# Two graph layers on one core: attention addends moved from TensorE transposes to a VectorE block transpose and two DMAs, row biases folded into beta, planner steps re-timed

## The chip, the core and the metric

The kernel runs on one core of a Trainium2 chip. The metric is the device time of one execution in microseconds. The kernel before took 3455.34 us, the median of three runs (3453.7 to 3455.74). The execution that was profiled took 3450.98 us; its trace spans 3449.2 us from the first to the last instruction.

## The reference

64 graphs of 256 nodes with 256 features go through two layers, all in fp32. Layer 0 is two graph attentions (GAT), a residual layernorm, and a feed-forward with relu. Layer 1 is attention with 8 heads whose values depend on the relation of the edge, and a feed-forward with gelu.

```python
def _gat(h, adj, W, a, out_features):
    Wh = jnp.matmul(h, W)
    Wh1 = jnp.matmul(Wh, a[:out_features])
    Wh2 = jnp.matmul(Wh, a[out_features:])
    e = jax.nn.leaky_relu(Wh1 + jnp.swapaxes(Wh2, 1, 2), negative_slope=ALPHA)
    att = jax.nn.softmax(jnp.where(adj > 0, e, NEG), axis=1)
    return jnp.matmul(att, Wh)
# layer 0
h = _gat(_gat(x, adj, W1, a1), adj, W2, a2)
h = _layernorm(x + h, g_ln1, b_ln1)
x = _layernorm(h + relu(h @ w_ff1 + b_ff1) @ w_ff2 + b_ff2, g_ln2, b_ln2)
# layer 1
attn = softmax((x @ Wq + bq) (x @ Wk + bk)^T / sqrt(32))     # per head
out = sum over r of (attn * (adj == r)) @ (x @ Wv[r] + bv[r])
x = _ln(x + out @ Wo + bo, g1, beta1)
x = _ln(x + gelu(x @ W1 + b1) @ W2 + b2, g2, beta2)
```

In a GAT layer, the weight of an edge comes from a sum of one number per row node and one per column node. The kernel calls these numbers the addends. Because exp(leaky_relu(s)) is the larger of exp(s) and exp(0.2 s), an unnormalised weight is the maximum of two products, each of a factor per row and a factor per column.

## The kernel before

**Tiling.** The 64 graphs are handled in 32 pairs. A pair has four row tiles of 128 nodes (index `k`, two per graph `b`). Each pair is a Python generator, `whole_way`, which emits the instructions of the pair in steps and yields between them. A feed-forward (`feed_forward`, L301) has eight steps that each make one 128x512 tile of the hidden layer (L308, two matmuls, with the activation at L311), and four quarters that multiply with the second weight (L319). A 128x512 fp32 matmul shows in the trace as two records.

**Order.** The order is written out by a small planner, `in_turn` (L151). Up to three pairs are under way. Each yield gives three things: the TensorE time of the step in us, the latency until the pair's next step may begin, and a stage that the next step needs. Three stages ("gat", "attention", "ff") are exclusive: only one pair may be in each. Among the pairs whose due time has come, those outside the feed-forward go first, so feed-forward steps fill the gaps. The costs in the yields only choose the order in which the program is written. On the chip each engine runs its own queue in order and waits at semaphores. The framework that assigns the semaphores may also shift an instruction against others in its engine's queue: the trace shows loads of `adjT` issued by SyncE ahead of an older output.

**The GAT stage** (`gat_layers`, L215). The projection (L227) of the pair's `xT` gives each row its 256 features and the addends in extra columns; ScalarE copies it to SBUF (L229). `addends` (L181) takes the largest absolute addend per graph (`steep`, a range check), and three exponentials on ScalarE: two of the row factor (`rise`, L189 and L190) and one of the ratio of the column factors (`ratio`, L191). `gat_weights` (L194) then needs the row factors along the free axis and on all partitions. Per graph, four TensorE transposes (L199) of a column broadcast to 128x128 put them into a PSUM bank; ScalarE copies half of it to `up` (L201); VectorE forms the maximum (L206), masks with the adjacency and sums (L207), takes the reciprocal (L209), and ScalarE scales the rows (L212). The product with the weights is L241 in the first GAT layer and L253 in the second. Then come residual and layernorm.

**Rows transposed** (`rows_transposed`, L294). Ahead of each feed-forward and of the attention, the rows are transposed on TensorE (L289), copied by ScalarE to `yT` (L290; two buffers), and GpSimd adds the bias of the coming sublayer to the rows (L292), so that the residual already holds it. The generator first takes the stage ("ff" or "attention") and then transposes.

**Layernorm** (`layernorm`, L268) is VectorE work, with the power -1/2 on GpSimd (L276).

**Transfers.** All are issued by SyncE: per pair `xT` (one buffer), `adjT` (four) and `x` (four) at L59 to L63, and the output at L456, which is written from the `x` tile. The load of the next pair is written right after the projection of the present one.

**Setup.** The weights are loaded to SBUF once; two small matmul groups (L119) fold the addend vectors into the first weight.

Of the kernel before, what the change touches and what calls it, by code (L numbers as in the profile page):

```python
# [29 lines left out]
def two_layers(ctx: ExitStack, tc: tile.TileContext, t: dict, out: bass.AP, flag: bass.AP):  # L30
# [25 lines left out]
    def load(pair):  # L56
        rows = slice(2 * pair, 2 * pair + 2)
        xT = io.tile([P, KC, 512], F32, name="xT")
        nc.sync.dma_start(xT, t["xT"][pair].rearrange("(c p) b n -> p c (b n)", p=P))  # L59
        adjT = io.tile([P, 4, N], I32, name="adjT", bufs=4)  # L60
        nc.sync.dma_start(adjT, t["adjT"][rows].rearrange("b (c p) n -> p (b c) n", p=P))
        x = io.tile([P, 4, D], F32, name="x", bufs=4)
        nc.sync.dma_start(x, t["x"][rows].rearrange("b (c p) d -> p (b c) d", p=P))  # L63
        return xT, adjT, x
# [13 lines left out]
    most = const.tile([P, NPAIR, 4], F32, name="most")  # L78
    steep = const.tile([P, NPAIR, 4], F32, name="steep")

# [23 lines left out]
    with tc.tile_pool(name="setup", bufs=1) as setup, \  # L104
            tc.tile_pool(name="psetup", bufs=2, space=bass.MemoryType.PSUM) as psetup:
        w1T, a2 = weights("L0_gnn_W1T", setup), on_all("L0_gnn_a2", 2 * D, setup)
        right = setup.tile([P, KC, D + 4], F32, name="right")
        nc.sync.dma_start(right[:, :, :D], t["L0_gnn_W2"].rearrange("(c p) m -> p c m", p=P))
        nc.sync.dma_start(right[:, :, D + 2:], t["L0_gnn_a1c"])
        junk = setup.tile([P, D], F32, name="junk")  # L110
        for s in range(2):
            for c in range(KC):
                nc.vector.scalar_tensor_tensor(
                    junk, right[:, c, :D], 1.0, a2[:, s * D:(s + 1) * D], op0=ALU.mult, op1=ALU.mult,
                    accum_out=right[:, c, D + s:D + s + 1])
        for m in range(KC):
            pw = psetup.tile([P, 512], F32, name="pw")
            for c in range(KC):
                nc.tensor.matmul(pw[:, :D + 4], lhsT=w1T[:, c, m * P:(m + 1) * P], rhs=right[:, c],  # L119
                                 start=c == 0, stop=c == KC - 1)  # L120
            nc.vector.tensor_copy(w12[:, m], pw[:, :D + 4])
    ln = [tuple(on_all(n, D) for n in names) for names in (
        ("L0_gnn_g_ln1", "L0_gnn_b_ln1"), ("L0_gnn_g_ln2", "L0_gnn_b_ln2"),
        ("L1_gnn_g1", "L1_gnn_beta1"), ("L1_gnn_g2", "L1_gnn_beta2"))]
    ff0 = (weights("L0_gnn_w_ff1"), column("L0_gnn_b_ff1"), weights("L0_gnn_w_ff2"), on_all("L0_gnn_b_ff2", D))
    wq, wk, wo = weights("L1_gnn_Wq"), weights("L1_gnn_Wk"), weights("L1_gnn_Wo")
    wv = const.tile([P, KC, 2, D], F32, name="wv")
    for c in range(KC):
        nc.sync.dma_start(wv[:, c], t["L1_gnn_Wv"][:2, c * P:(c + 1) * P, :].rearrange("r p m -> p r m"))
        nc.vector.tensor_tensor(wv[:, c, 1], wv[:, c, 1], wv[:, c, 0], ALU.subtract)  # L130
    bq, bk = column("L1_gnn_bq"), column("L1_gnn_bk")
    bqs = const.tile([P, KC], F32, name="bqs")
    nc.vector.tensor_scalar(bqs, bq, SCALE, None, ALU.mult)
    bv, bo = on_all("L1_gnn_bv", 2 * D), on_all("L1_gnn_bo", D)
    nc.vector.tensor_tensor(bv[:, D:], bv[:, D:], bv[:, :D], ALU.subtract)
    ff1 = (weights("L1_gnn_W1"), column("L1_gnn_b1"), weights("L1_gnn_W2"), on_all("L1_gnn_b2", D))

    work = ctx.enter_context(tc.tile_pool(name="work", bufs=1))
    small = ctx.enter_context(tc.tile_pool(name="small", bufs=6))
    psum = ctx.enter_context(tc.tile_pool(name="psum", bufs=8, space=bass.MemoryType.PSUM))  # L140

# [38 lines left out]

    def addends(y, at, layer, pair, b):  # L181


        k = of_graph(b)
        nc.vector.tensor_reduce(steep[:, pair, 2 * layer + b:2 * layer + b + 1], y[:, k, at:at + 2], axis=AX.XY,
                                op=ALU.max, apply_absolute_value=True)
        e1, e2 = y[:, k, at], y[:, k, at + 1]
        rise, ratio = small.tile([P, 2, 2], F32, name="rise"), small.tile([P, 2], F32, name="ratio")
        nc.scalar.activation(rise[:, 0], e1, AF.Exp, bias=shift[:, 0:1])  # L189
        nc.scalar.activation(rise[:, 1], e1, AF.Exp, bias=shift[:, 0:1], scale=ALPHA)  # L190
        nc.scalar.activation(ratio, e2, AF.Exp, scale=ALPHA - 1.0)  # L191
        return rise, ratio

    def gat_weights(y, at, rise, ratio, adjT, empty, b):  # L194

        p = bank()
        for n in range(4):
            col = rise[:, n // 2, n % 2:n % 2 + 1]
            nc.tensor.transpose(p[:, n * P:(n + 1) * P], col.to_broadcast([P, P]), ident)  # L199
        up = work.tile([P, N], F32, name="up", bufs=2)  # L200
        nc.scalar.activation(up, p[:, :N], AF.Copy)  # L201
        e = work.tile([P, 2, N], F32, name="e", bufs=4)
        sums, rs = small.tile([P, 2], F32, name="sums"), small.tile([P, 2], F32, name="rs")
        for j in range(2):
            k = 2 * b + j
            nc.vector.scalar_tensor_tensor(e[:, j], p[:, N:], ratio[:, j:j + 1], up, op0=ALU.mult, op1=ALU.max)  # L206
            nc.vector.scalar_tensor_tensor(e[:, j], adjT[:, k], empty[:, k:k + 1], e[:, j],  # L207
                                           op0=ALU.max, op1=ALU.min, accum_out=sums[:, j:j + 1])
# [6 lines left out]
    def gat_layers(pair, xT, adjT, x):  # L215
# [4 lines left out]
        z = work.tile([P, 4, D + 4], F32, name="xw", bufs=2)  # L220
        a, e = [], []
        for b in range(2):
            for j in range(2):
# [5 lines left out]
                nc.scalar.activation(y[:, k], ps[:, :D + 4], AF.Copy)  # L229
            a.append(addends(y, D + 2, 0, pair, b))  # L230
            yield 1.75, b * 1.6, None
        if pair + 1 < NPAIR:
            loaded[pair + 1] = load(pair + 1)
        for b in range(2):
            e.append(gat_weights(y, D + 2, *a.pop(0), adjT, empty, b))
            yield 0.5, b * 3.4, None
        for b in range(2):
            for i in range(2):
# [4 lines left out]
                nc.scalar.activation(z[:, 2 * b + i, :D + 2], ps[:, :D + 2], AF.Copy)  # L243
            a.append(addends(z, D, 1, pair, b))
            yield 1.75, 0.4 + b * 0.6, None
        for b in range(2):
            e.append(gat_weights(z, D, *a.pop(0), adjT, empty, b))
            yield 0.5, b * 3.4, None
        for b in range(2):
# [9 lines left out]
        done_with("gat")  # L259
        yield 1.75, 4.5, "ff"  # L260

# [21 lines left out]

    def transposed(y, yT, bias, b):

        pt = bank()
        for c in range(KC):
            for j in range(2):
                nc.tensor.transpose(pt[:, c * N + j * P:c * N + (j + 1) * P], y[:, 2 * b + j, c * P:(c + 1) * P], ident)  # L289
        nc.scalar.activation(yT[:, :, b * N:(b + 1) * N], pt.rearrange("p (c n) -> p c n", c=KC), AF.Copy)  # L290
        for j in range(2):
            nc.gpsimd.tensor_tensor(y[:, 2 * b + j, :], y[:, 2 * b + j, :], bias, ALU.add)  # L292

    def rows_transposed(y, bias):  # L294
        yT = work.tile([P, KC, 512], F32, name="yT", bufs=2)
        for b in range(2):
            transposed(y, yT, bias, b)
            yield 0.5, 0.5 + b * 0.5, None
        return yT

    def feed_forward(y, w, func, gb):  # L301
        w1, b1, w2, b2 = w
        yT = yield from rows_transposed(y, b2)
        f = []
# [40 lines left out]
    def attention(y, pair, adjT):  # L345


        yT = yield from rows_transposed(y, bo)
        qT, kT, oT = (work.tile([P, KC, 512], F32, name=n) for n in ("qT", "kT", "oT"))

# [73 lines left out]
        for n, (b, c) in enumerate(groups):  # L424
# [9 lines left out]
            divided(b, c, po)  # L434
            yield 3.1 if last else 4.1, 3.2 if last else 0.8, None
            if (b, c) == (0, KC - 1):
# [8 lines left out]
        done_with("attention")  # L445
        yield 1.75, 4.5, "ff"

    def whole_way(pair):
        yield 0.0, 0.0, "gat"
        xT, adjT, x = loaded.pop(pair)  # L450
        yield from gat_layers(pair, xT, adjT, x)
        yield from feed_forward(x, ff0, AF.Relu, ln[1])
        yield 3.44, 4.5, "attention"
        yield from attention(x, pair, adjT)
        yield from feed_forward(x, ff1, AF.Gelu, ln[3])
        nc.sync.dma_start(out[2 * pair:2 * pair + 2].rearrange("b (c p) d -> p (b c) d", p=P), x)  # L456
        yield 3.44, 0.0, None

    in_turn((whole_way(pair) for pair in range(NPAIR)), 3)


    ranges = ((reach, NPAIR * 4, N * SAFE), (most, NPAIR * 4, 1.0), (steep, NPAIR * 4, STEEP))
    count = const.tile([P, len(ranges)], F32, name="count")
# [405 lines left out]

_COLUMNS = ("L0_gnn_b_ff1", "L1_gnn_bq", "L1_gnn_bk", "L1_gnn_b1")  # L870


# [24 lines left out]
```

## Time and profile before

| quantity | value |
|---|---|
| median of 3 runs | 3455.34 us |
| profiled execution, and its span | 3450.98 us, 3449.2 us |
| granted TensorE clock | 0.999 |
| TensorE busy | 3344.4 us (97%) |
| VectorE, ScalarE, GpSimd busy | 1904.6, 1371.0, 481.5 us |
| DMA traffic over the span | 22 GB/s |
| activation table loads on ScalarE | 218 of 1283 ns |

How to read it: busy times are the union of the spans of an engine's instructions. Matmuls are pipelined, so a matmul's own duration is longer than the spacing at which the next one follows; where two rows of the timeline follow without a gap, the difference of their starts is the time that counts. In a list of groups, the figures are busy time, mean duration of one, then the idle time of that engine just before them and what ended it. A wait for several semaphores is put down to the one that came last.

### The profile page before, as it was taken

How to read it: one execution, taken by the hardware profiler on the slowest of the kernel's cores; microseconds unless marked ns; L12 is line 12 of the kernel's file. 1: busy time of each engine (PE TensorE's matmuls, PEld its weight loads, DVE VectorE, ACT ScalarE, POOL GpSimd, SP SyncE). 2: the span in 40 equal slices, each digit the busy share in tenths (PEclk: the TensorE clock that was granted, in tenths of full speed). 3: DMA queues.
4: the chain of work that ended last, by engine and by line, in shares of the span. 5: the costliest groups of instructions: out<-in, count | busy, mean ns of one | idle time of the engine just before them, and what ended most of it. 6: DMA issues, size and time to landing. Idle time of an engine off the chain costs nothing.

```text
span 3449.2 us, 47284 instructions
## 1 busy us (share of the span) xinstructions
PE 3344.4 (97%) x18698; PEld 2150.5 (62%) x18698; DVE 1904.6 (55%) x4825; ACT 1371.0 (40%) x2586; POOL 481.5 (14%) x646
## 2 busy tenths in 40 slices
PE   7999999999999999999999999999999999999998
PEld 5566665666656566565665666656666566565655
DVE  5655645556456564555645555465554655546455
ACT  4343343433434334343444434444253442534332
POOL 0201111011110111111111111111111111111110
PEclk9999999999999999999999999999999999999999
DMA  5000010000100001000000100001000010000000
GB/s 166 7 25 19 13 37 7 25 19 13 37 7 25 25 7 37 7 28 23 20 25 7 41 10 25 19 7 43 7 25 19 7 43 7 25 19 1 13 1 14
DMA packets 66868, 78.22 MB, mean 23 GB/s; under 512 B 3280, under 2 KB 57680, under 8 KB 66640
## 3 DMA queue, kind: packets, MB, share of 16 engines
q1 hardware_dynamic: 66640, 75.13, 7.0%
q8 instruction: 150, 2.46, 0.3%
q14 instruction: 78, 0.64, 0.1%
HBM read 58.34 MB, written 16.78 MB: 22 GB/s over the span
## 4 chain that ended last, share of the span: by engine, by line
PE 87%; ACT 9%; DVE 2%; DMA 1%; issue 0%; SPq 0%; POOL 0%; POOLq 0%; DVEq 0%
PE ps L319 26%; PE ps L308 23%; PE ps L342 7%; PE ps L335 6%; PE ps L388 6%; PE ps L360 4%; PE ps L381 4%; PE ps L253 3%; PE ps L405 3%; ACT L189 2%; ACT yT L290 2%; PE ps L241 2%; PE ps L227 2%; PE ps L289 1%; ACT ff L311 1%; DVE e L206 1%
## 5 line engine op out<-in xcount | busy, mean ns | idle before, releaser
L276 POOL TENSOR_TENSOR rstd<-rstd,mhalf 128x2 f32<-128x2 f32 x256 | 206.1, 805 | 2729.3 <-DVE rstd L275 2713.4
L308 PE MATMUL ps<-yT,w_L_gnn_W 128*128 128x512 f32 x1024 | 482.7, 602 | 14.2 <-ACT yT L290 12.5
L308 PE MATMUL ps<-yT,w_L_gnn_w_ff 128*128 128x512 f32 x1024 | 482.5, 602 | 14.1 <-ACT yT L290 12.5
L319 PE MATMUL ps<-w_L_gnn_w_ff,ff 128*128 128x256 f32 x2048 | 450.2, 379 | 0.0
L319 PE MATMUL ps<-w_L_gnn_W,ff 128*128 128x256 f32 x2048 | 449.9, 379 | 0.0
L319 PEld LDWEIGHTS ps<-w_L_gnn_W,ff 128*128 128x128 f32 x2048 | 389.1, 190 | 66.6 <-issue 15.3
L319 PEld LDWEIGHTS ps<-w_L_gnn_w_ff,ff 128*128 128x128 f32 x2048 | 389.0, 190 | 66.0 <-issue 14.8
L374 DVE TENSOR_TENSOR m<-a,adjT 128x512 f32<-128x512 f32 x512 | 327.0, 688 | 175.6 <-ACT a L365 134.9
L266 DVE TENSOR_TENSOR x<-ps,x 128x512 f32<-128x512 f32 x256 | 176.1, 688 | 444.3 <-PE ps L319 330.7
L311 ACT ACTIVATE ff<-ps,c_L_gnn_b_ff 128x512 f32<-128x512 f32 x256 | 176.0, 687 | 448.2 <-PE ps L308 448.2
L365 ACT ACTIVATE a<-ps 128x512 f32<-128x512 f32 x512 | 264.4, 602 | 216.3 <-PE ps L360 216.1
L337 DVE TENSOR_TENSOR v<-ps,b_L_gnn_bv 128x512 f32<-128x512 f32 x128 | 88.1, 689 | 400.5 <-PE ps L335 400.5
L308 PEld LDWEIGHTS ps<-yT,w_L_gnn_W 128*128 128x128 f32 x1024 | 183.0, 190 | 199.2 <-issue 174.1
L308 PEld LDWEIGHTS ps<-yT,w_L_gnn_w_ff 128*128 128x128 f32 x1024 | 183.1, 190 | 198.9 <-issue 174.2
L290 ACT ACTIVATE yT<-ps 128x512 f32<-128x512 f32 x192 | 110.2, 592 | 479.8 <-PE ps L289 479.8
L311 ACT ACTIVATE ff<-ps,c_L_gnn_b 128x512 f32<-128x512 f32 x256 | 175.9, 687 | 292.8 <-PE ps L308 292.4
L335 PE MATMUL ps<-wv,yT 128*128 128x512 f32 x512 | 235.4, 592 | 0.0
L229 ACT ACTIVATE xw<-ps 128x260 f32<-128x260 f32 x128 | 45.7, 379 | 456.0 <-PE ps L227 456.0
L394 DVE RECIPROCAL s<-ps 128x256 f32<-128x256 f32 x128 | 224.0, 1750 | 0.0
L273 DVE BATCH_NORM_STATS2 st<-x 128x6 f32<-128x256 f32 x512 | 192.7, 418 | 8.6
L206 DVE SCALAR_TENSOR_TENSOR e<-ps,ratio,up 128x256 f32<-128x256 f32 x256 | 115.7, 475 | 141.2 <-ACT up L201 141.2
L335 PEld LDWEIGHTS ps<-wv,yT 128*128 128x128 f32 x512 | 97.3, 190 | 122.5 <-issue 122.2
(81 smaller groups left out, 4290.1 us busy)
## 6 DMA issues: line engine op xcount, KB each, us to landing
xT<-in_xT SPq DMA_DIRECT2D x32, 512.0 KB, 4.6
adjT<-in_adjT SPq DMA_DIRECT2D x32, 512.0 KB, 3.9
x<-in_x SPq DMA_DIRECT2D x32, 512.0 KB, 4.2
out<-x SPq DMA_DIRECT2D x32, 512.0 KB, 3.2
w_L_gnn_w_ff<-in_L_gnn_w_ff SPq DMA_DIRECT2D x2, 1024.0 KB, 11.3
w_L_gnn_W<-in_L_gnn_W SPq DMA_DIRECT2D x2, 1024.0 KB, 7.0
wv<-in_L_gnn_Wv SPq DMA_DIRECT2D x2, 256.0 KB, 7.1
w_L_gnn_W1T<-in_L_gnn_W1T SPq DMA_DIRECT2D x1, 256.0 KB, 6.1
```

The lines of the kernel that those rows point to most:

```text
L273: nc.vector.bn_stats(st[:, j, :], r[:, 2 * b + j, :])
L276: nc.gpsimd.tensor_tensor(rstd, rstd, mhalf[:, :2], ALU.pow)
L290: nc.scalar.activation(yT[:, :, b * N:(b + 1) * N], pt.rearrange("p (c n) -> p c n", c=KC), AF.Copy)
L308: nc.tensor.matmul(p1, lhsT=w1[:, c, m * P:(m + 1) * P], rhs=yT[:, c, :], start=c == 0, stop=c == KC - 1)
L311: nc.scalar.activation(h, p1, func, bias=b1[:, m:m + 1])
L319: nc.tensor.matmul(p2[:, j * D:(j + 1) * D], lhsT=f[m][:, k * P:(k + 1) * P], rhs=w2[:, m, :], start=m == 0, stop=m == NF - 1)
L335: nc.tensor.matmul(ps, lhsT=yT[:, c, at:at + P], rhs=wv[:, c].rearrange("p r m -> p (r m)"), start=c == 0, stop=c == KC - 1)
L342: nc.tensor.matmul(ps, lhsT=w[:, d, c * P:(c + 1) * P], rhs=yT[:, d, :], start=d == 0, stop=d == KC - 1)
L365: nc.scalar.activation(a, ps[o], AF.Exp)
L374: nc.vector.tensor_tensor(m, a, adj, ALU.mult)
L388: nc.tensor.matmul(po[o * DH:(o + 1) * DH, :N], lhsT=v[:, jc, at:at + DH], rhs=ms[o][:, jc * N:(jc + 1) * N], start=r == 0 and jc == 0, st ...
L394: nc.vector.reciprocal(s, po[:, N:])
```

## The change

Five things are edited together.

- **Addends.** Both graphs of the pair are handled by one call. The four row factors are written into a 128x64 tile (`rise`, two of them, cleared once), VectorE transposes it in 32x32 blocks, a first DMA writes 4 KB of the result to a DRAM scratch tile, and a second DMA reads them back onto all 128 partitions (`rows`, 4 KB on each). `gat_weights` reads `rows` in place of PSUM and of `up`. The four TensorE transposes and the ScalarE copy per graph are gone.
- **Row biases.** The three row biases are added to the beta of the layernorm in front, at setup. What else reads those rows would then see the bias too, so it is taken out of the biases of the readers (`b1`, `bq`, `bk`, `bv`) with small matmuls at setup. GpSimd's adds per pair are gone.
- **Row transposes** no longer need the stage; it is asked for after them. `yT` has three buffers.
- **Latencies** in the yields are changed, and the weights steps cost no TensorE time.
- **Loads.** The next pair's load is written after the second layer's addends, `x` has five buffers, and the output is written one yield later.

```diff
-        x = io.tile([P, 4, D], F32, name="x", bufs=4)
+        x = io.tile([P, 4, D], F32, name="x", bufs=5)
...
+        for n, (name, readers) in enumerate((("L0_gnn_b_ff2", ((ff0[0], ff0[1]),)),
+                                             ("L1_gnn_bo", ((wq, bq), (wk, bk))),
+                                             ("L1_gnn_b2", ((ff1[0], ff1[1]),)))):
+            beta = ln[n][1]
+            nc.vector.tensor_tensor(beta, beta, on_all(name, D, setup), ALU.add)
+            b = setup.tile([P, KC], F32, name="c_" + name)
+            nc.sync.dma_start(b, t[name + "c"])
+            for w, bias in readers:
+                pw = psetup.tile([P, 512], F32, name="pw")
+                of = w.shape[-1] // P
+                for m in range(of):
+                    for c in range(KC):
+                        nc.tensor.matmul(pw[:, m:m + 1], lhsT=w[:, c, m * P:(m + 1) * P], rhs=b[:, c:c + 1],
+                                         start=c == 0, stop=c == KC - 1)
+                nc.vector.tensor_tensor(bias, bias, pw[:, :of], ALU.subtract)
...
+        rise, ratio = rises[layer], small.tile([P, 4], F32, name="ratio")
+        of_kind = rise.rearrange("p j (n s) -> p n j s", n=4)[:, :, :, 0]
+        for b in range(2):
+            e1 = y[:, of_graph(b), at]
+            nc.scalar.activation(of_kind[:, 2 * b], e1, AF.Exp, bias=shift[:, 0:1])
+            nc.scalar.activation(of_kind[:, 2 * b + 1], e1, AF.Exp, bias=shift[:, 0:1], scale=ALPHA)
+        nc.scalar.activation(ratio, y[:, :, at + 1], AF.Exp, scale=ALPHA - 1.0)
+        blocks = small.tile([P, 2, 32], F32, name="blocks")
+        nc.vector.transpose(blocks.rearrange("p j c -> p (j c)"), rise.rearrange("p j c -> p (j c)"))
+        row = scratch.tile([2, 16, 32], F32, name="row")
+        nc.sync.dma_start(row.rearrange("j q c -> q j c"), blocks[0:P:8])
+        rows = work.tile([P, 8, 4, 32], F32, name="rows", bufs=2)
+        nc.sync.dma_start(rows.rearrange("p q n c -> p (q n c)"), row.rearrange("j q c -> (j q c)").partition_broadcast(P))
...
-        p = bank()
-        for n in range(4):
-            col = rise[:, n // 2, n % 2:n % 2 + 1]
-            nc.tensor.transpose(p[:, n * P:(n + 1) * P], col.to_broadcast([P, P]), ident)
-        up = work.tile([P, N], F32, name="up", bufs=2)
-        nc.scalar.activation(up, p[:, :N], AF.Copy)
...
-            nc.vector.scalar_tensor_tensor(e[:, j], p[:, N:], ratio[:, j:j + 1], up, op0=ALU.mult, op1=ALU.max)
+            nc.vector.scalar_tensor_tensor(e[:, j].rearrange("p (q c) -> p q c", q=8), rows[:, :, 2 * b + 1],
+                                           ratio[:, k:k + 1], rows[:, :, 2 * b], op0=ALU.mult, op1=ALU.max)
...
-            a.append(addends(y, D + 2, 0, pair, b))
-            yield 1.75, b * 1.6, None
-        if pair + 1 < NPAIR:
-            loaded[pair + 1] = load(pair + 1)
-        for b in range(2):
-            e.append(gat_weights(y, D + 2, *a.pop(0), adjT, empty, b))
-            yield 0.5, b * 3.4, None
+            if b == 0:
+                yield 1.75, 0.0, None
+        rows, ratio = addends(y, D + 2, 0, pair)
+        yield 1.75, 8.6, None
+        e = [gat_weights(y, D + 2, rows, ratio, adjT, empty, b) for b in range(2)]
+        yield 0.0, 4.6, None
...
+        rows, ratio = addends(z, D, 1, pair)
+        if pair + 1 < NPAIR:
+            loaded[pair + 1] = load(pair + 1)
+        yield 1.75, 8.6, None
+        e += [gat_weights(z, D, rows, ratio, adjT, empty, b) for b in range(2)]
+        yield 0.0, 4.6, None
...
-        yield 1.75, 4.5, "ff"
+        yield 1.75, 6.0, None
...
+    def rows_transposed(y, needs):
+
+        yT = work.tile([P, KC, 512], F32, name="yT", bufs=3)
         for b in range(2):
-            transposed(y, yT, bias, b)
-            yield 0.5, 0.5 + b * 0.5, None
+            pt = bank()
...
+            yield 0.5, 0.5 + b * 0.8, needs if b else None
...
-        yield 3.44, 4.5, "attention"
+        yield 3.44, 6.0, None
         yield from attention(x, pair, adjT)
         yield from feed_forward(x, ff1, AF.Gelu, ln[3])
+        yield 3.44, 5.0, None
         nc.sync.dma_start(out[2 * pair:2 * pair + 2].rearrange("b (c p) d -> p (b c) d", p=P), x)
-        yield 3.44, 0.0, None
```

In the attention, the step after the last group of heads is told 4.8 us in place of 3.2, and the feed-forward behind the attention 6.0 us and no stage in place of 4.5 us and "ff".

## The prediction

> **What bounds the kernel now.** I read the top of the page first, then the busy time of each engine in stretches, then TensorE's waits, then TensorE's timeline, and last the rows that price the pieces.
>
> ```profile
> span 3449.2 us, 47284 instructions
> ...
> PE 3344.4 (97%) x18698; PEld 2150.5 (62%) x18698; DVE 1904.6 (55%) x4825; ACT 1371.0 (40%) x2586; POOL 481.5 (14%) x646
> ```
>
> TensorE is busy for 97%, and no other engine for more than 55%. So only two things can shorten the run: less streaming on TensorE, or fewer gaps. The gaps are 3449.2 - 3344.4 = 104.8 us. Busy time by stretches shows where they lie (first column the stretch, then its length and PE's busy time):
>
> ```profile
> 0.00:45.20 45.20, 25.09 (x105) 18.95 (x105) 21.77 (x75) 15.50 (x47) 4.71 (x12) 0.96 0.93 287
> ...
> 439.00:652.40 213.40, 208.53 (x1170) 134.16 (x1169) 118.50 (x300) 85.96 (x163) 29.89 (x41) 1.00 0.07 21
> ```
>
> The first 45.2 us, up to the first feed-forward matmul, hold 20.1 us of idle. After that the work repeats every 213.4 us, which is two pairs of graphs (106.7 us each), and each period has 4.87 us of idle. TensorE's waits over the run name them (total us, times, longest):
>
> ```profile
> PE ps L199 <- ACT rise L189: 29.6, 46, 0.9
> PE ps L308 <- ACT yT L290: 25.0, 34, 0.7
> PE ps L253 <- ACT xw L212: 21.0, 16, 3.0
> PE pw L119 <- DVE junk L113: 11.4, 1, 11.4
> ```
>
> All but L119 recur per pair: the transposes of the addend columns (L199) wait for ScalarE's exponentials, the feed-forward (L308) for the copy of its transposed rows, the GAT product (L253) for the scaled rows. TensorE's timeline over one GAT stage shows them in place:
>
> ```profile
> 1078.45 1.04 PE L289 MATMUL ps<-ident,x 128*128 128x128 f32 x8
> 1079.32 0.60 PE L199 MATMUL ps<-ident,rise 128*128 128x128 f32 x4
> 1080.44 0.65 PE L199 MATMUL ps<-ident,rise 128*128 128x128 f32 x4 [0.52 <-ACT rise L189]
> 1081.21 3.70 PE L308 MATMUL ps<-yT,w_L_gnn_W 128*128 128x512 f32 x8
> ...
> 1091.66 0.60 PE L199 MATMUL ps<-ident,rise 128*128 128x128 f32 x4
> 1093.18 0.65 PE L199 MATMUL ps<-ident,rise 128*128 128x128 f32 x4 [0.92 <-ACT rise L189]
> ```
>
> Starts matter here, not durations: eight L289 transposes last "1.04", but the next group starts 0.87 after them. A transpose occupies the stream for 0.109 us, and the remaining 0.17 us is a drain that overlaps the next work, or is lost in front of a gap.
>
> **What the skill says.** "TensorE: Matmul & The Clock Gate", Part 4, gives about 275 ns for a PE transpose inside a kernel and says that access latency dominates it. The trace agrees in duration (76.3 us of union over 512, 277 ns mean in the PE groups), but the price of taking one away is the spacing, 0.109 us. "DMA: Bandwidth & Descriptors", Two DMAs through the same engine are not ordered: the second of the two new DMAs has to wait for the first one's completion, so their latencies add. No run here shows this yet. The same page, Latency and other measured facts, puts a DMA's fixed cost near 2 us, mostly the write receipt; the 512 KB output here lands in 3.2 us, which fits. "ScalarE: Activation LUTs", What ACT_TABLE_LOAD costs: 1283 ns; the trace has 1283 too. (Prices used below besides: a VectorE 128x128 transpose, 311 ns for bf16, "VectorE: DVE Perf Modes", The three transpose paths.)
>
> ```profile
> adjT<-in_adjT SPq DMA_DIRECT2D x32, 512.0 KB, 3.9
> x<-in_x SPq DMA_DIRECT2D x32, 512.0 KB, 4.2
> out<-x SPq DMA_DIRECT2D x32, 512.0 KB, 3.2
> ```
>
> **The change, part by part.** The sum is made against the profiled execution, 3450.98 us (span 3449.2 and 1.8 around it). The median of the runs, 3455.34, is 4.4 above it.
>
> *Transposes out of TensorE.* 4 transposes x 2 graphs x 2 layers x 32 pairs = 512, at 0.109 us: **-55.7 us**, all on the bounding engine. The 128 `up` copies (42.7 us of ScalarE) and 64 of 128 `ratio` exponentials go too; ScalarE is busy for 40%, so they count only through waits.
>
> *The steady gaps.* 4.87 us per period, plus the drain lost in front of each gap (19 waits in the 650 us from 800 to 1450, so 6.2 per period, x 0.17 = 1.06), is 5.93, or 2.97 per pair. The L199 wait goes with its instructions. The L290 wait goes because the rows are transposed before the stage is free, behind other steps (third `yT` buffer). The L212 wait goes because the planner is told 4.6 us between weights and product and fills it. Over about 31 pairs: **-92 us**. This leaves 106.7 - 2.97 - 16 x 0.109 = 102.0 us per pair.
>
> *What comes late next.* The new chain, from the end of the projection to the first product: ACT copy 0.39, table load 1.28, five exponentials at their spacing of 0.19 (1.05 with the last), maximum 0.15 and transpose 0.25 on VectorE (between the 0.15 of the small reduction and the 0.31 of the page), first DMA 2.5 (4 KB; between the page's 2.0 and the 3.2 of the 512 KB output), second DMA 4.0 (512 KB into SBUF; the loads take 3.9 and 4.2; bounds 3.2 and 5.5 with other traffic), then two L206, two L207, reciprocal and two L212 for the first graph, 3.1. Sum 12.7. I walked the planner's rule with the new costs for the order of the steps only. In the steady order, five L308 steps and two quarters of L319 stand between the first layer's addends and its product: 5 x 1.72 + 2 x 3.45 = 15.5 us of cover. A load of `xT` becomes due at the same moment (the projection frees its buffer) and is 1.4 us of transfer at the 370 GB/s of the start: 14.1, still covered; a layernorm half on VectorE (about 3 us) in front would uncover 1.6. In the second layer some 30 us of the next attention's first steps are cover. But there the row scaling (L212) stands on ScalarE behind the rows' landing, and the feed-forward's activation and the next attention's `yT` copies queue behind it. By the same sums the rows land about 9.3 us after the projection while these activations come from 8 us on, so up to 1.7 us reaches TensorE at the first attention projection. I take 0.4 for the first place and 0.9 for the second, 1.3 per pair (bounds 0.3 and 5): 31 x 1.3 = **+40 us**.
>
> *SyncE's queue.* Per pair four small issues of about 0.4 us come in. They'd be stuck if they stood behind a waiting transfer. The `adjT` wait (L61) and the output wait (L456) make up nearly all of SP's waiting before. In the new order the output is issued before the next pair's projection, told 8.4 us after its layernorm; the `adjT` and `x` buffers of a new load (x now has five) are free long before. I cost this at 0, because those 8.4 us cover the layernorm (about 4 us); if the output were late it would hold both row DMAs back.
>
> *Biases into beta.* 192 x 2 POOL adds go, 276 us of POOL, which waits 2729 us in front of its power operation (L276): 0 on the path, as no chain that TensorE waits for goes through them. In exchange 42 setup matmuls (84 records) come, at 0.109 to 0.19 each: 9 to 16 us, with weights as their cover at the start.
>
> *Start and end.* The first pair has no feed-forward to hide behind. Before, its first L308 starts at 45.2. Now two chains lie open. If its projection still runs at 15.8 us while the weights load (landings then take 4 to 11 us, so 14 for two instead of 6.5): 19.5 + 20 + 3.7 + 13 + 3.6 + a layernorm 4 + transposes and copy 1.5 = 66. If it has to stand behind the setup matmuls, whose last weights land after 35 us, the same sum starts at 37 to 45 and ends at 79 to 87. So +21 to +42; I take **+32**. The longer latencies at the last pair: **+4**.
>
> Sum: -55.7 - 92 + 40 + 32 + 4 = -71.7, so 3379 in the profiled execution and **3384 us** in the median.
>
> **Rivals.** (1) *Row chain late, slower.* Mechanism: TensorE takes its steps in order, so each product L241 waits if the rows land after the cover. With 3 us of layernorm ahead of the transpose, 1.5 us more in each DMA by traffic, and the ScalarE block of 1.7, the stall is 12.7 + 1.4 + 3 + 3 - 15.5 = 4.6, plus 1.7: about 6 per pair, less what doesn't coincide, 5. It decides from (147.7 - 36)/31 = 3.6 us per pair on. At 5: 3384 + 31 x 3.7 = 3499. For it: two dependent DMAs in a row where VectorE is 55% busy. Against: 1.4 to 2.8 us to spare by durations. (2) *Gaps only change names.* New stalls equal the old, 2.6 per pair: 3384 + 40 = 3424. For it: the old latencies were also told, and still 4.87 us remained per period. (3) *No new stall* (0.3) and the short start (21), no end cost: 3379 - 31 - 11 - 4 + 4 = 3337. A measurement of this kernel can tell about 0.2% (7 us) from no change. That the removed transposes don't shorten TensorE's stream I exclude, as they aren't overlapped by other matmuls in the timeline.
>
> **How the numbers follow.** Forecast (3362 to 3408) 0.60; rival 2 (3408 to 3448) 0.20; rival 3 0.07; rival 1 0.13. The range 3345 to 3440 leaves out rival 1, the lower half of rival 3 and the top of rival 2, 0.18 in all. Faster 0.84, within 0.2% 0.04, slower 0.12.
>
> **What would show it.** Right: the period (pair) falls from 106.7 to about 103.3; L199 is gone from TensorE's groups; the rows' second DMA lands in about 4 us; the waits of L308 for `yT` nearly vanish; first L308 near 77. Wrong: a wait of L241 for L212 of over 2 us per pair, or the row DMAs on SyncE behind an output or a load (rival 1); as many gaps at the attention's first projections as there were at L199 (rival 2).

## The result, and the profile after

The changed kernel takes **3457.1 us** (median of 4 runs, 3455.7 to 3458.5), the kernel before 3454.5 us beside it (3451.5 to 3455.7). The ratio of the times is 1.0009, with an interval of 0.9991 to 1.0026: no difference that can be measured. The forecast was 3384, with a range of 3345 to 3440, so the result lies outside it.

The top of the page of the kernel after:

```profile
span 3455.4 us, 45656 instructions
...
PE 3323.7 (96%) x18270; PEld 2129.3 (62%) x18270; DVE 1843.1 (53%) x4835; ACT 1261.9 (37%) x2326; POOL 202.9 (6%) x262
```

The work did go away: 428 matmul records fewer (512 transposes out, 84 setup matmuls in), 260 fewer on ScalarE, 384 fewer on GpSimd. But the span is 6 us longer, and TensorE's idle time grew from 104.8 to 131.7 us. And its busy time fell by 20.7 us only, where the transposes alone were 55.7 and the setup matmuls add 9 to 16: the rest must have become slower. The mean granted clock says so: 0.983, where it was 0.999.

TensorE's waits over the run (total us, times, longest):

```profile
PE ps L418 <- DVE v L367: 66.1, 47, 2.4
PE pw L155 <- DMA b_L_gnn_bo<-in_L_gnn_bo: 18.1, 1, 18.1
PE pw L123 <- DVE junk L117: 11.9, 1, 11.9
PE ps L272 <- ACT xw L245: 10.8, 1, 10.8
PE ps L287 <- ACT xw L245: 9.3, 1, 9.3
...
PE ps L338 <- ACT yT L327: 1.4, 2, 0.7
```

All the steady waits of before are gone. The feed-forward's wait for `yT` (L338, formerly L308) fell from 25.0 to 1.4 us, the GAT products L272 and L287 wait once each, at the start. One new wait has taken their place: the attention's product of weights and values, L418, waits for `v`, which VectorE copies with its bias at L367. The prediction names no such wait.

47 waits in 32 pairs are neither one nor two per pair. The output DMAs, as SyncE's timeline shows them, tell why (start us, duration):

```profile
1990.10 0.39 SPq L487 DMA_DIRECT2D out<-x  x1
2096.82 0.39 SPq L487 DMA_DIRECT2D out<-x  x1
2203.19 0.39 SPq L487 DMA_DIRECT2D out<-x  x1
2305.72 0.39 SPq L487 DMA_DIRECT2D out<-x  x1
```

The distance is 106.7 and 106.4 us, and then 102.5. It stays at 102.5 for all 11 distances after 2203.19. In the 18 before it, values of 106.4 to 106.7 and of 107.8 alternate, with a mean of 106.9, as slow as before the change (106.7). So the run has two halves. One period from each, as stretches (stretch, length, busy time of PE, PEld, DVE, ACT, POOL, then granted clock, DMA share, GB/s):

```profile
1669.20:1776.00 106.80, 103.59 (x569) 66.14 (x568) 57.37 (x151) 38.76 (x73) 6.32 (x8) 0.98 0.10 30
2203.20:2305.70 102.50, 101.74 (x569) 65.40 (x568) 57.20 (x150) 40.79 (x75) 6.31 (x8) 1.00 0.10 32
```

The same 569 matmul records take 101.74 us in one and 103.59 in the other. The 4.3 us between the periods are 2.45 of idle (3.21 against 0.76) and 1.85 of slower matmuls. TensorE's timeline shows both in place, first in the slow half (start us, us, operation, in brackets the idle time before it):

```profile
661.94 2.00 PE L287 MATMUL ps<-xw,e 128*128 128x256 f32 x8
663.77 3.60 PE L365 MATMUL ps<-wv,yT 128*128 128x512 f32 x8
667.29 1.15 PE L390 MATMUL ps<-qT,kT 32*128 32x256 f32 x16
668.37 1.07 PE L411 MATMUL ps<-a,ones 128*32 128x256 f32 x16
670.30 0.64 PE L418 MATMUL ps<-a,v 128*32 128x256 f32 x8 [0.86 <-DVE v L367]
673.29 1.08 PE L418 MATMUL ps<-a,v 128*32 128x256 f32 x8 [2.35 <-DVE v L367]
674.14 1.93 PE L418 MATMUL ps<-m,v 128*32 128x256 f32 x16
676.01 1.12 PE L325 MATMUL ps<-ident,x 128*128 128x128 f32 x4
676.91 2.92 PE L338 MATMUL ps<-yT,w_L_gnn_W 128*128 128x512 f32 x4
```

The values (L365) are followed at once by scores, sums and the products that need them. TensorE waits 0.86 us for the first half of `v` and 2.35 us for the second. Then everything is slow for a while: sixteen L418 records last 1.93 us where others of that shape last 1.05, four transposes 1.12 where others last 0.60. The stretch from 675 to 679 has a granted clock of 0.50:

```profile
675.00:679.00 4.00, 4.00 (x19) 2.12 (x12) 2.84 (x3) 1.82 (x2) 0.00 (x0) 0.50 0.14 15
```

The trace records a half clock in each of these 18 pairs, beginning between 1.2 us before and 1.3 us after the end of the second wait. It lasts 3.4 us, and in every third pair 6.8 us, which is the longer period of 107.8. VectorE's timeline of the same moment shows why `v` is late:

```profile
659.23 0.63 DVE L300 TENSOR_TENSOR x<-ps,x 128x512 f32<-128x512 f32 x1
...
665.96 1.75 DVE L424 RECIPROCAL s<-ps 128x256 f32<-128x256 f32 x1
667.62 0.63 DVE L300 TENSOR_TENSOR x<-ps,x 128x512 f32<-128x512 f32 x1
...
669.58 0.66 DVE L367 TENSOR_TENSOR v<-ps,b_L_gnn_bv 128x512 f32<-128x512 f32 x1
...
671.75 0.88 DVE L316 SCALAR_TENSOR_TENSOR x<-x,rstd,b_L_gnn_b_ln 128x256 f32<-128x256 f32 x2 [0.58 <-POOL rstd L310]
672.55 0.69 DVE L367 TENSOR_TENSOR v<-ps,b_L_gnn_bv 128x512 f32<-128x512 f32 x1
```

Ahead of the second bias add of L367 stand a reciprocal of 1.75 us and the residual and layernorm of the second graph's GAT output (L300 to L316), which themselves wait for GpSimd's power (L310). The same work for the first graph stands there too, one group of heads earlier (L300 at 659.23). In the fast half both GAT products (L287) stand one group of heads later, so the second one comes behind the products L418 that wait, and of the two waits one of 0.76 us remains:

```profile
2368.93 3.60 PE L365 MATMUL ps<-wv,yT 128*128 128x512 f32 x8
...
2374.42 0.61 PE L418 MATMUL ps<-a,v 128*32 128x256 f32 x8
2375.79 0.64 PE L418 MATMUL ps<-a,v 128*32 128x256 f32 x8 [0.76 <-DVE v L367]
...
2377.22 2.00 PE L287 MATMUL ps<-xw,e 128*128 128x256 f32 x8
```

VectorE's timeline there:

```profile
2368.46 1.75 DVE L424 RECIPROCAL s<-ps 128x256 f32<-128x256 f32 x1
...
2375.05 0.68 DVE L367 TENSOR_TENSOR v<-ps,b_L_gnn_bv 128x512 f32<-128x512 f32 x1
```

From this reciprocal to the second bias add the queue is the same in both halves, a layernorm included, and takes 6.59 us in both. The difference is when it starts: 2.19 us after TensorE begins the values (L365) in the slow half, 0.47 us before that in the fast half. In the slow half VectorE comes to it later, since it has the residuals and layernorms of two graphs to do in this stretch, where the fast half has one.

The counts fit: 18 pairs with two waits of 3.21 together, and 11 with one of 0.76, are 47 waits and 66.1 us.

**Why there are two halves.** It is the planner's arithmetic. The first GAT layer is told 8.6 us between addends and weights, and a feed-forward step costs 1.72, so five steps are exactly 8.6. The planner's question `g[1] <= now` (L191) is then a tie, and rounding decides. Its sums, followed through, do this: up to a planner clock of 2048, five additions of 1.72 reach the due time in every repeating pair. In the 22nd pair the clock passes 2048, where the sum carries fewer digits behind the point, and from there on it falls 9e-13 short. The weights step then comes one step later, and each of the second layer's two products moves behind the next group of heads: the first from behind group 0 to behind group 1, the second from behind group 1, ahead of the values, to behind group 2.

The start: busy time up to the first feed-forward matmul (granted clock 0.84), and TensorE's timeline there:

```profile
0.00:98.00 98.00, 44.87 (x165) 36.17 (x165) 26.42 (x89) 13.69 (x38) 2.43 (x8) 0.84 0.51 157
```

```profile
33.87 6.96 PE L155 MATMUL pw<-c_L_gnn_b_ff,w_L_gnn_w_ff 128*128 128x1 f32 x32 [18.10 <-DMA b_L_gnn_bo<-in_L_gnn_bo]
...
51.62 6.79 PE L259 MATMUL ps<-w,xT 128*128 128x260 f32 x16 [0.26 <-DVE c_L_gnn_b L157]
69.20 6.51 PE L272 MATMUL ps<-xw,e 128*128 128x258 f32 x16 [10.79 <-ACT xw L245]
...
85.04 5.41 PE L287 MATMUL ps<-xw,e 128*128 128x256 f32 x16 [9.32 <-ACT xw L245]
...
97.99 10.55 PE L338 MATMUL ps<-yT,w_L_gnn_w_ff 128*128 128x512 f32 x20 [0.69 <-ACT yT L327]
```

The first feed-forward matmul starts at 98.0 us instead of 45.2. The projection stands behind the setup matmuls until 51.62, and then two chains of addends lie open, of 10.8 and 9.3 us. The projection takes 6.79 us where it takes 3.67 in the steady part; the granted clock from 51.6 to 58.4 is 0.55.

### The profile page after: what moved, and what is told of

Same layout as the page of the kernel before. It is cut to its first block, busy times and chain, and to the rows that moved or that the text cites. A ratio compares the mean times of both kernels' runs of the same rounds, so it can differ in the third digit from the quotient of the medians.

```text
span 3455.4 us, 45656 instructions
## 1 busy us (share of the span) xinstructions
PE 3323.7 (96%) x18270; PEld 2129.3 (62%) x18270; DVE 1843.1 (53%) x4835; ACT 1261.9 (37%) x2326; POOL 202.9 (6%) x262
## 4 chain that ended last, share of the span: by engine, by line
PE 84%; DVE 10%; issue 1%; POOL 1%; DMA 1%; ACT 1%; SPq 0%; DVEq 0%; POOLq 0%
PE ps L338 26%; PE ps L349 26%; PE ps L372 6%; PE ps L418 5%; PE ps L365 3%; PE ps L272 3%; PE ps L435 3%; PE ps L259 3%; PE ps L325 3%; PE ps L390 3%; DVE s L424 2%; DVE m L404 2%; PE ps L411 2%; POOL rstd L310 1%; DVE x L316 1%
## 5 line engine op out<-in xcount | busy, mean ns | idle before, releaser
L338 PE MATMUL ps<-yT,w_L_gnn_W 128*128 128x512 f32 x1024 | 476.9, 603 | 0.7 <-ACT yT L327 0.7
L349 PE MATMUL ps<-w_L_gnn_W,ff 128*128 128x256 f32 x2048 | 457.9, 380 | 0.0
L338 PE MATMUL ps<-yT,w_L_gnn_w_ff 128*128 128x512 f32 x1024 | 452.4, 595 | 0.7 <-ACT yT L327 0.7
L349 PEld LDWEIGHTS ps<-w_L_gnn_w_ff,ff 128*128 128x128 f32 x2048 | 390.0, 190 | 65.3 <-issue 14.8
L300 DVE TENSOR_TENSOR x<-ps,x 128x512 f32<-128x512 f32 x256 | 172.7, 675 | 418.7 <-PE ps L349 326.5
L310 POOL TENSOR_TENSOR rstd<-rstd,mhalf 128x2 f32<-128x2 f32 x256 | 202.2, 790 | 3246.0 <-DVE rstd L309 3232.3
L338 PEld LDWEIGHTS ps<-yT,w_L_gnn_w_ff 128*128 128x128 f32 x1024 | 193.0, 191 | 216.8 <-issue 206.8
L338 PEld LDWEIGHTS ps<-yT,w_L_gnn_W 128*128 128x128 f32 x1024 | 188.7, 196 | 181.4 <-issue 174.3
L238 DVE SCALAR_TENSOR_TENSOR e<-rows,ratio 128x256 f32<-128x256 f32 x256 | 116.5, 478 | 281.8 <-DMA rows<-row 251.4
L367 DVE TENSOR_TENSOR v<-ps,b_L_gnn_bv 128x512 f32<-128x512 f32 x128 | 87.2, 682 | 286.8 <-PE ps L365 286.8
L365 PE MATMUL ps<-wv,yT 128*128 128x512 f32 x512 | 235.4, 592 | 0.0
L418 PE MATMUL ps<-a,v 128*32 128x256 f32 x2048 | 146.6, 395 | 66.1 <-DVE v L367 66.1
L365 PEld LDWEIGHTS ps<-wv,yT 128*128 128x128 f32 x512 | 97.5, 190 | 109.9 <-issue 103.6
```

Of the source, the lines that this page charges most:

```text
L300: nc.vector.tensor_tensor(rows, p, rows, ALU.add)
L310: nc.gpsimd.tensor_tensor(rstd, rstd, mhalf[:, :2], ALU.pow)
L338: nc.tensor.matmul(p1, lhsT=w1[:, c, m * P:(m + 1) * P], rhs=yT[:, c, :], start=c == 0, stop=c == KC - 1)
L349: nc.tensor.matmul(p2[:, j * D:(j + 1) * D], lhsT=f[m][:, k * P:(k + 1) * P], rhs=w2[:, m, :], start=m == 0, stop=m == NF - 1)
L365: nc.tensor.matmul(ps, lhsT=yT[:, c, at:at + P], rhs=wv[:, c].rearrange("p r m -> p (r m)"), start=c == 0, stop=c == KC - 1)
L418: nc.tensor.matmul(po[o * DH:(o + 1) * DH, :N], lhsT=v[:, jc, at:at + DH], rhs=ms[o][:, jc * N:(jc + 1) * N], start=r == 0 and jc == 0, st ...
```

## The experiments

The theory: VectorE's queue ahead of L367 costs the 18 pairs 4.4 us each, by late values and the half clock that follows, through an order that a tie picks. Rival theories: the half clock comes by itself or from another cause; the row chain's DMAs or the longer latencies cost the time; the start alone is to blame.

**e1_tie_up.** One digit of the planner's numbers, so that five steps never reach the due time.

```diff
-        yield 1.75, 8.6, None
+        yield 1.75, 8.6001, None
```

> The changed kernel with one number edited: the first GAT layer's latency is told as 8.6001 in place of 8.6. Five feed-forward steps of 1.72 are exactly 8.6, so the planner's choice rests on rounding; with 8.6001 all 29 middle pairs get the order that only the last 11 have (weights after three quarters of the feed-forward's second half, the second GAT products after the second head group). Theory A (the order puts the GAT layernorm on VectorE ahead of the values' bias add, TensorE waits 3.2 us and then runs a stretch at half clock): 18 pairs fall from 107.0 to 102.5, so 3457 - 80 = 3377 us, and the half-clock stretches in the middle vanish. Rival B (the pairs after 2185 us are faster for a reason that depends on time in the run, such as the clock): no change, 3457. Rival C (the row chain by two DMAs is what costs): no change, 3457.

Measured 3382.0 us, ratio to before 0.9788 (0.9772 to 0.9805). A middle period as a stretch, and the wait over the run:

```profile
1500.00:1602.50 102.50, 101.75 (x569) 65.25 (x569) 57.13 (x151) 40.83 (x74) 6.32 (x8) 1.00 0.10 32
```

```profile
PE ps L418 <- DVE v L367: 22.2, 29, 1.1
```

Nearly every pair in the middle takes 102.5 us (26 of the 29 distances between outputs; the others are 102.9 to 103.1), with one wait of 0.77. One ten-thousandth of a microsecond in a planner's number is worth 75 us on the chip.

**e2_tie_down.** The same digit the other way, so that five steps always reach it.

```diff
-        yield 1.75, 8.6, None
+        yield 1.75, 8.5999, None
```

> The changed kernel with 8.5999 in place of 8.6: all 29 middle pairs get the order of the first 18. Theory A: 11 pairs rise from 102.5 to 107.0, 3457 + 49 = 3506 us, and half-clock stretches run to the end. Rivals B and C: 3457.

Measured 3506.2 us, ratio 1.0153 (1.0136 to 1.017). A late period as a stretch, and the wait over the run:

```profile
3000.00:3106.90 106.90, 103.70 (x571) 65.77 (x570) 57.84 (x153) 39.32 (x75) 6.23 (x8) 0.98 0.09 30
```

```profile
PE ps L418 <- DVE v L367: 92.8, 58, 2.4
```

Two waits per pair, 3.2 us together, to the end of the run, and the half clock in each pair. The kernel after lies between e1 and e2 as its 18 and 11 pairs say: 18/29 of the way from 3382 to 3506.2 is 3459, and 3457.1 was measured. So it is shown that the order alone makes the difference between the halves.

**e3_fill.** In e2's order, four matmuls whose result nobody reads fill the gap ahead of L418. This leaves the computation as it is and adds 3.4 us of work per pair.

```diff
+            if n == 2:
+                spare = bank()
+                for _ in range(4):
+                    nc.tensor.matmul(spare, lhsT=yT[:, 0, :P], rhs=yT[:, 0, :], start=True, stop=True)
```

> As with 8.5999, and in front of the products of the third head group four extra 128x512 matmuls into a bank that nobody reads (3.44 us of TensorE), which fill the time in which TensorE waits for the values. Theory A with the half clock caused by that gap: the wait of L418 is gone, the half clock too (2.3 us a pair on average), 0.24 us of extra matmul stays: about 104.9 a pair, 3447 us. If the half clock has another cause: 107.2 a pair, 3513.

Measured 3469.9 us, ratio 1.0046 (1.0029 to 1.0063), 36 us below e2 with more work in it. A middle period, and TensorE's timeline around the fill (L463):

```profile
1500.00:1605.20 105.20, 105.20 (x584) 66.68 (x576) 57.37 (x151) 38.76 (x73) 6.31 (x8) 1.00 0.10 31
```

```profile
2041.00 3.70 PE L463 MATMUL ps<-yT 128*128 128x512 f32 x8
2044.63 1.07 PE L418 MATMUL ps<-a,v 128*32 128x256 f32 x16
```

TensorE has no idle time in the period, its clock is 1.00, and the sixteen L418 records behind the fill take 1.07 us. So the half clock follows from the two waits: with these filled it doesn't occur in the pairs. The period was forecast well (104.9). The total is 23 us above the forecast, of which 9.3 lie at the start (first output at 286.8 instead of 277.5 us) and 3.5 at the end; the rest is 0.3 us per pair.

**e4_v_act.** In e2's order, the values are copied by ScalarE, so that they don't stand in VectorE's queue. The value bias is left out.

```diff
-        nc.vector.tensor_tensor(v[:, jc], ps, bv, ALU.add)
+        nc.scalar.activation(v[:, jc], ps, AF.Copy)
```

> As with 8.5999, but ScalarE copies the values from PSUM to SBUF in place of VectorE's add; the value bias is left out. Theory A (VectorE's queue is the cause, not where the products stand on TensorE): no wait of L418, no half clock, about 102.1 a pair in spite of the old order, 3506 - 29 x 4.9 = 3364 us. If it were the order on TensorE itself: about 3506.

Measured 3390.9 us, ratio 0.9818 (0.9801 to 0.9834). TensorE's largest wait, and a middle period:

```profile
PE ps L435 <- DVE oT L428: 33.6, 26, 1.5
```

```profile
1500.00:1603.00 103.00, 101.73 (x570) 65.28 (x569) 54.70 (x146) 41.18 (x76) 6.31 (x8) 1.00 0.10 32
```

The wait at L418 and the half clock in the pairs are gone, 115 us against e2, with TensorE's order unchanged. So it is shown that the values are late because they stand in VectorE's queue. Which piece of that queue would have to go was not tried. But it was 27 us above the forecast: the same queue now makes itself felt one step later, at the projection of the heads (L435), which waits 1.3 us per pair for VectorE's L428. The start also stayed longer at half clock, 41 us.

**e5_moved.** The start: e1 with the setup matmuls moved behind the first pair's addends.

```diff
+    def fold(n):
+        b, (name, readers) = columns[n], folded[n]
...
+        if pair == 0:
+            fold(0)
...
+        if pair == 0:
+            fold(1)
+            fold(2)
```

> The kernel with 8.6001, and the small setup matmuls of the row biases moved out from in front of the first pair: they are written behind the first pair's addends, in the same PSUM banks as all other work, and the row biases are added to beta early. Theory A (about a third of the loss at the start is the first pair's projection standing behind the setup matmuls and the last weights): the projection runs at 16 us in place of 55, the first feed-forward matmul at about 72 in place of 101.6 (the first row DMA still stands behind the weights on SyncE), 3382 - 30 = 3352 us. Rival (the start is bound by the two row chains and the weights' loading alone): 3382.

Measured 3357.9 us, ratio 0.9724 (0.9708 to 0.974), 24 us below e1. TensorE's timeline at the start:

```profile
38.19 6.99 PE L167 MATMUL ps<-c_L_gnn_b_ff2c,w_L_gnn_w_ff 128*128 128x1 f32 x32 [16.09 <-DMA c_L_gnn_b_ff2c<-in_L_gnn_b_ff2c]
```

The projection now runs at 16.3 us, and the first feed-forward matmul at 79.6 instead of 101.6 (e1). Forecast was 72: the moved matmuls waited another 16.1 us for the bias columns, which land behind the weights.

**e6_unbias.** The other way out: e1 with the row biases added by GpSimd, as before the change, and so without setup matmuls (`x` has four buffers again).

```diff
+            for j in range(2):
+                nc.gpsimd.tensor_tensor(y[:, 2 * b + j, :], y[:, 2 * b + j, :], bias, ALU.add)
```

> The kernel with 8.6001 and the row biases as before the change: GpSimd adds them after each row transpose, no setup matmuls (x has four buffers, for lack of space). Theory A: GpSimd's adds are off every chain, and the start falls as in the run before, 3382 - 30 = 3352 us. Rival (taking the adds off GpSimd and VectorE's neighbours is a gain of its own): the pair grows by 0.5 us or more, 3367 or above.

Measured 3359.5 us, ratio 0.9728 (0.9712 to 0.9744). A middle period (GpSimd's busy time is the fifth):

```profile
1500.00:1602.50 102.50, 101.49 (x568) 65.08 (x567) 58.59 (x150) 40.73 (x74) 15.28 (x20) 1.00 0.10 32
```

GpSimd works 15.28 us per pair instead of 6.32, and the period is the same 102.5. The fold of the row biases gains nothing in the steady part. It costs 22.5 us of the total, through the start: the first feed-forward matmul comes at 76.1 us without it, at 101.6 with it (e1).

**e7_petr.** e1 with the addend rows by TensorE transposes and a ScalarE copy, so that only the rest of the change remains.

```diff
+        p = bank()
+        for n in range(4):
+            col = rows[:, 2 * b + n // 2, n % 2:n % 2 + 1]
+            nc.tensor.transpose(p[:, n * P:(n + 1) * P], col.to_broadcast([P, P]), ident)
+        up = work.tile([P, N], F32, name="up", bufs=2)
+        nc.scalar.activation(up, p[:, :N], AF.Copy)
```

> The kernel with 8.6001 and the new order, but the addend rows made as before the change: four TensorE transposes and one ScalarE copy per graph and layer, no DMA. Theory A (each transpose takes 0.109 us of TensorE's stream; the old waits for the exponentials are hidden by the told 8.6 us): 3382 + 56 - 10 for the shorter chains at the start = 3428 us. Rival (the DMA route gains nothing, all of the gain is the order): 3372.

Measured 3416.3 us, ratio 0.9892 (0.9875 to 0.9908). A middle period:

```profile
1500.00:1604.10 104.10, 103.55 (x586) 67.18 (x585) 56.16 (x149) 42.75 (x79) 6.32 (x8) 1.00 0.07 21
```

104.1 us per pair: the rest of the change, with the tie out of the way, brings 106.7 to 104.1, and the route by VectorE and DMA brings another 1.6. Which part of the rest brings the 2.6 was not separated, except that the fold of the biases brings none of it (e6). But the first feed-forward matmul starts at 88.1 here, 13.5 earlier than in e1. So the route gains 31 x 1.6 = 50, loses 13.5 where nothing covers it, and 36 remain; 34 was measured.

**e8_both.** e5, and the planner is told 2 us after the second graph's values, so that it puts a GAT product and a feed-forward step between them and the products.

```diff
-                    yield 1.72, 0.0, None
+                    yield 1.72, 2.0 * jc, None
```

> As the kernel with the moved setup matmuls, and the second values step of the second graph tells 2.0 us of latency in place of 0, so that the planner puts a GAT product and a feed-forward step between the values and the third head group. Theory A: the last 0.76 us a pair of waiting for the values goes, 3352 - 21 = 3331 us, under both kernels. Rival (the GAT layernorm then meets the head group's work on VectorE and moves the wait elsewhere): 3352.

Measured 3337.8 us, ratio 0.9665 (0.9649 to 0.9681). A middle period:

```profile
1500.00:1601.50 101.50, 101.50 (x570) 65.37 (x569) 57.63 (x151) 43.51 (x76) 6.31 (x8) 1.00 0.10 32
```

TensorE is busy for the whole period, 101.5 us. Over the distances between outputs this gained 27 us. The end took 9.3 us longer than in e5, behind the thirtieth output. The trace shows why: nothing is left there to cover the last attention's layernorm. TensorE waits 5.55 us for it at the row transposes (L330, for VectorE's L321), where e5 has a feed-forward quarter in between, and then runs at half clock: the 32 records of the last feed-forward's first half (L343) take 16.7 us there, 13.8 in e5.

**e9_first_pair.** e8, and the first pair, which has no work to hide its chains behind, takes its rows by TensorE transposes; the bias columns are loaded ahead of the weights, and the other setup matmuls come behind its last GAT product.

```diff
+        if pair == 0:
+            return rise, ratio
...
+    columns = [column(name + "c") for name in ("L0_gnn_b_ff2", "L1_gnn_bo", "L1_gnn_b2")]
```

> As the kernel with the moved setup and the told latency of the values, and for the first pair alone the addend rows by TensorE transposes, as before the change; the small columns are loaded ahead of the weights, and the second and third fold stand behind the first pair's last GAT product. Theory A (what is left of the loss at the start is two open DMA chains and a wait for a small column behind the weights on SyncE): the first feed-forward matmul at about 55 us in place of 78.7, 3338 - 24 = 3314 us. Rival (the weights' loading bounds the start anyway): no change, 3338.

Measured 3325.2 us, ratio 0.9627 (0.9614 to 0.964), 3.7% below the kernel before. TensorE's timeline at the start:

```profile
32.28 5.70 PE L287 MATMUL ps<-xw,e 128*128 128x258 f32 x16 [2.69 <-ACT xw L258]
```

The chain ahead of the first product leaves idle times of 2.25 us (ahead of its transposes) and 2.69 us instead of the 10.8 of the changed kernel, and the first feed-forward matmul starts at 63.5. Forecast was 55: sixteen product records still take 5.70 us, at a granted clock of 0.65. That TensorE's gaps keep the clock down there is likely, but no run shows it.

## Why the prediction was wrong, by its own steps

**Transposes out of TensorE, -55.7: right.** e1 against e7 has 1.6 us per pair, where 16 x 0.109 = 1.7 was set down.

**The steady gaps, -92: right as far as it goes.** The three waits it names are gone from the steady part, and where no new one stands the period falls below the 103.3 us forecast: 102.5, and 101.5 in e8, against a floor of 102.0.

**What comes late next, +40: this is the step that failed.** "I take 0.4 for the first place and 0.9 for the second, 1.3 per pair". Both places were wrong, in the good direction: the row chain takes 10.9 us in the steady part (end of the projection 603.85, scaled rows 614.72; 12.7 was set down) and the product starts at 619.17, so 4.5 us were left over. The cover of 15.5 us that was set down is also the one in the trace (603.68 to 619.17). There is no wait at the attention's first projections (L372). The stall came at a third place, the products L418, because the order that the new latencies make sets the GAT layernorms of both graphs on VectorE close together ahead of the values. I had walked the planner's rule for the order of steps, found where the rows are needed, and never asked of the new order what each other engine's queue holds in front of TensorE's next operand. Nor did the walk see that five steps of 1.72 are exactly the 8.6 told. In 18 pairs this cost 3.2 us of waits each, where 1.3 was set down, and some 2 us more in matmuls slowed by the half clock that the waits set off. The prediction's steps have no term for the clock. That the total came out level with the kernel before is chance: it rests on where the planner's rounding turned. With one order throughout, the same change is 1.5% slower (e2) or 2.1% faster (e1).

The two DMAs were forecast well enough. Their rows on the page (size, median from issue to landing):

```profile
rows<-row SPq DMA_DIRECT2D x64, 512.0 KB, 3.7
row<-blocks SPq DMA_DIRECT2D x64, 4.0 KB, 1.8
```

2.5 and 4.0 were taken. The near 2 us of fixed cost that the prediction quoted agrees with the 1.8 us of the 4 KB. **SyncE's queue, 0**, was right: in 61 of 64 cases SyncE was at the first row DMA (L227) early and waited for VectorE's transpose. **Biases into beta, 0 in the steady part**, was right too (e6).

**Start, +32: too small; it was +52.8.** The branch "behind the setup matmuls" was the right one, with 79 to 87 as its end; 98.0 was measured. The projection started at 51.6 instead of 37 to 45, as the 84 setup records took 17.5 us instead of 9 to 16 (48 of them 0.21 each). The projection and the two products took 6.79, 6.51 and 5.41 us where 3.7, 3.7 and 3.6 were set down: here too the clock had no term. The chains themselves were shorter than set down, with 10.8 and 9.3 us of idle for 12.7 and 13.

The sum: 18 pairs at 106.9 - 103.3 = 3.6 give +64.8, 11 pairs at 102.5 - 103.3 give -8.8, the start +20.8. Together +76.8, of the 77.9 us between the forecast 3379.3 and the 3457.2 of the profiled execution.

Two small slips in the working change nothing: by its own pieces the rows land 9.6 us after the projection, not 9.3, and the short start adds up to 65.3, not 66. And the wait of L253, said to recur per pair, occurs 16 times in 32 pairs.

**The rivals.** Rival 2 ("gaps only change names") is nearest, but it set the new stalls at 2.6 per pair and at places that didn't stall. Rival 1 (row chain late) is refuted: 4.5 us to spare. Rival 3 (no new stall) is what e8 shows in the middle, with 101.5 us per pair, under the 102.0 set down.

## What to carry to other kernels

When a change moves steps in a written order, read the queue of every engine in the new order, not only that of the engine that the change relieves: the late operand may come from a queue that the change didn't touch. Ask too how late that queue comes to the work: here the same 6.59 us stood in it in both halves, and only its start moved. Numbers that a planner compares should not be exact multiples of each other; give them a margin, and see from the distances between outputs whether all periods are alike. A latency that is hidden in the steady part is paid in full in the first pass, so the first pass may deserve its own route.

## What the runs showed of the hardware

The Trainium skill, "TensorE: Matmul & The Clock Gate", section Why this matters for your kernels, advises against idle gaps of more than about 3 us between matmul bursts, as one window of idle brings the clock to half. The half clock agrees: 0.50, here for 3.4 us at a time, or for 6.8 in the five pairs in which it began more than 1 us before the second wait ended. The limit for a gap doesn't: here gaps of 0.86 and 2.35 us, with eight matmul records between them, sufficed in all 18 pairs of the kernel after and in every middle pair of e2. Together they are 3.2 us of idle within 3.9 us. A single gap of 0.76 us per pair never did (e1), nor one of 1.3 (e4). Where between these the limit lies was not tried.

A VectorE transpose of 128x64 elements in 32x32 blocks took 0.245 us. Reading 4 KB of DRAM onto all 128 partitions (512 KB landed) took 3.7 us, no more than the loads of distinct 512 KB in the same run (3.9 to 4.1).
